# A branch hint for the branch over the general path of a graph network kernel

## The chip, the cores and the metric

The kernel runs on one core of a Trainium2 chip. A core has five engines with a sequencer each: TensorE (PE: matmuls, with its weight loads shown apart as PEld), VectorE (DVE), ScalarE (ACT), GpSimd (POOL) and SyncE (SP, which here only starts DMAs and waits). Each runs its own list of instructions and meets the others through semaphores. [...] The metric is the device time of one execution, in microseconds.

## What is computed

A layer norm with ReLU, then three layers of edge convolution on a graph of 2500 nodes and 80000 edges (the edges are sorted by destination), then one product of all layers' features with a last matrix:

```python
h = relu(layernorm(x))                    # x: 2500 x 256, float32
xs = [h]
for W, b in three layers:                 # W: 512 x 256
    xi, xj = h[dst], h[src]
    m = concatenate([xi, xj - xi]) @ W + b          # one row for each edge
    s = segment_sum(m, dst); cnt = segment_sum(1, dst)
    h = relu(s / maximum(cnt, 1))
    xs.append(h)
out = x + concatenate(xs) @ Wf + bf
```

## The kernel before

The sums over edges are written as products with a matrix of counts, how many edges lead from node m to node n. `by_windows` (line 314) builds this matrix: it takes the destinations in windows of 6 nodes, assumes that a window has at most 256 edges and that a pair of nodes has few edges in common, and compares the edges' node numbers with a running index (`one_m`, `one_n`) to get the counts by matmuls of zeros and ones. The counts go to HBM as bf16 (`a_dram`) for the later layers. Layer 0 is done while the counts are built; layers 1 and 2 stream the counts back (`staged`) and use a scheme of seven products for two pairs of groups of columns. Products that need float32 accuracy are made of two or three reduced products (`zh`, `zl`, `sh`, `sl`, and the forms of `Split` and `Forms`).

The order of the work is written out by hand. A class `InOrder` (line 272) issues through its line 282, so nearly every instruction of the profile has that line; names of tiles tell them apart. At the end (lines 1399 to 1417) ten pairs of node tiles get their last product; VectorE adds it to `acc` (`add_to_acc`), and `out` is written from `acc`, by SP's queue, and twice by ScalarE's, among them the very last write.

The assumptions on the edges may not hold for other inputs. In the first layer VectorE compares the number of edges found with the true one and sets the flag `missing` to 0 or 1. After `by_windows`, `gnn_kernel` loads the flag into a register of every engine (line 1425), each engine branches on it (line 1426), and where it is 1 the whole result is computed anew by `general` (line 17), which assumes nothing. With the inputs of the reference the flag is 0, and no instruction of `general` is in the profile.

In the built program the branch stands behind the last instruction of `by_windows` in the list of each engine. It has two targets: the first instruction of `general`, which comes next in line, and the code behind `general`. The skipped code has 2056 instructions on TensorE, 1780 on VectorE, 275 on ScalarE, 1016 on GpSimd and 139 on SyncE. Behind it each engine has semaphore instructions that end the branch's region (line 1426), and then the closing meeting of all engines (line 1450): each finishes with a DRAIN and reports to GpSimd, which clears the semaphores when all are there.

## Time and profile before

| | us |
|---|---|
| median of three executions | 478.93 (478.14 to 479.45) |
| the profiled execution's own time | 478.33 |
| span of the profile, from the first to the last instruction | 476.4 |
| TensorE busy with matmuls | 463.5 (97%) |
| VectorE busy | 380.9 (80%) |
| ScalarE busy | 310.8 (65%) |
| GpSimd busy | 42.7 (9%) |
| code brought in: 23 packets, 0.38 MB, and 22 packets, 0.18 MB | |

The profile page gives sums and the chain of work that ended last. Instructions of the sequencers alone (branches, register loads, semaphore instructions, DRAINs) are not counted as busy and are not in the chain; a view by source line lists them, with the shortest, median and longest duration in nanoseconds and the first and last start in microseconds from the span's start. A `q` behind an engine's name marks its sequencer or its DMA queue. DMA packets that carry code have the kind "instruction".

### The profile page before, as it was taken

The page shows a single profiled execution, that of the slowest core. Times are in us where ns is not written, and L with a number is a line of the kernel's source. Part 1 is how long each engine was busy: PE and PEld are TensorE (multiplying, and loading weights), DVE is VectorE, ACT ScalarE, POOL GpSimd, SP SyncE. Part 2 cuts the span into 40 slices and gives each one's busy share as a digit, 9 for nine tenths or more (in the row PEclk, how much of TensorE's full clock was granted, in tenths as well). Part 3 has the DMA queues.
Part 4 walks back from the last instruction along what each step waited for, and adds up shares of the span by engine and source line. Part 5 has one row for each costly group of instructions (what it writes and reads, how often), then busy time and mean ns, then how long its engine had stood idle before and what let it go on. Part 6 is the DMA issues. An engine that isn't in the chain of part 4 may idle for free.

```text
span 476.4 us, 7357 instructions
## 1 busy us (share of the span) xinstructions
PE 463.5 (97%) x2739; PEld 365.9 (77%) x2739; DVE 380.9 (80%) x699; ACT 310.8 (65%) x543; POOL 42.7 (9%) x66
## 2 busy tenths in 40 slices
PE   8999999999999999999999999999999999999992
PEld 4787888787877888868887867877788787687691
DVE  8988988799898872599986848876999685669883
ACT  5776687685754441577869858766877886587330
POOL 2664014300101001000000000000000000000000
PEclk9999999999999999999999999999999999999997
DMA  8310084990824608441187542011124764120032
GB/s 279 96 46 1 1 163 70 193 216 14 178 42 89 131 1 179 95 131 43 45 291 258 182 160 89 1 44 45 43 54 158 289 207 151 77 88 0 1 128 95
DMA packets 21779, 52.11 MB, mean 109 GB/s; under 512 B 1943, under 2 KB 12134, under 8 KB 21734
## 3 DMA queue, kind: packets, MB, share of 16 engines
q1 hardware_dynamic: 14662, 33.67, 21.5%
q0 software_dynamic: 5856, 16.51, 18.1%
q10 hardware_dynamic: 1216, 1.37, 0.9%
q8 instruction: 23, 0.38, 0.3%
q14 instruction: 22, 0.18, 0.1%
HBM read 36.08 MB, written 15.46 MB: 108 GB/s over the span
## 4 chain that ended last, share of the span: by engine, by line
PE 86%; DVE 7%; POOL 2%; DMA 2%; issue 1%; SPq 0%; DVEq 0%; POOLq 0%
PE bank L282 82%; PE pz L282 3%; DVE acc L282 2%; DMA acc<-in_x_dram 2%; POOL acc L282 1%; DVE staged L282 1%; DVE st L282 1%; POOL es L282 1%; DVE zl L282 0%; POOL ed L282 0%; DVE mv L282 0%; DVE tmp L282 0%; PE turned L282 0%; DVE rs L282 0%; DVE kn L282 0%
## 5 line engine op out<-in xcount | busy, mean ns | idle before, releaser
L282 ACT CAST block<-staged 128x1008 fp32r<-128x1008 bf16 x120 | 117.8, 1032 | 17.1 <-DVE staged L282 6.3
L282 PE MATMUL bank<-block,zh 128*128 128x504 f32 (+1 forms) x200 | 83.7, 419 | 0.0
L282 PE MATMUL bank<-a,zh 128*128 128x504 f32 (+1 forms) x200 | 81.7, 409 | 0.0
L282 ACT CAST a<-bank 128x480 fp32r<-128x480 f32 (+1 forms) x105 | 54.5, 561 | 39.0 <-PE bank L282 37.1
L282 PE MATMUL bank<-a,zl 128*128 128x504 f32 (+1 forms) x200 | 77.8, 389 | 0.0
L282 PE MATMUL bank<-block,zl 128*128 128x504 f32 (+1 forms) x200 | 77.3, 387 | 0.0
L282 DVE TENSOR_TENSOR one_m<-iota_m,key_m 128x2048 bf16<-128x2048 bf16 (+2 forms) x55 | 64.3, 1169 | 9.9 <-PE bank L282 9.7
L282 PE MATMUL bank<-block,sh 128*128 128x504 f32 x160 | 69.0, 431 | 0.0
L282 PE MATMUL bank<-block,staged 128*128 128x512 f32 (+1 forms) x312 | 67.2, 365 | 0.6 <-DVE staged L282 0.5
L282 PE MATMUL bank<-block,sl 128*128 128x504 f32 x160 | 62.6, 391 | 0.0
L282 PEld LDWEIGHTS bank<-block,staged 128*128 128x128 f32 x312 | 52.3, 188 | 11.9 <-DVE staged L282 2.1
L282 DVE TENSOR_TENSOR one_n<-iota_n,key_n 128x960 bf16<-128x960 bf16 (+2 forms) x110 | 51.4, 508 | 0.0
L282 DVE TENSOR_TENSOR block<-staged 128x1008 fp32r<-128x1008 bf16 x40 | 46.9, 1204 | 5.5 <-PE bank L282 4.2
L282 PEld LDWEIGHTS <-one_m 128*128 128x128 bf16 x834 | 37.4, 97 | 13.6 <-issue 7.6
L282 PEld LDWEIGHTS bank<-block,zh 128*128 128x128 f32 x200 | 37.6, 188 | 10.8 <-issue 2.5
L282 PEld LDWEIGHTS bank<-block,zl 128*128 128x128 f32 x200 | 37.6, 188 | 10.6 <-issue 3.5
L282 PE MATMUL bank<-one_n,one_m 128*128 128x120 bf16 x834 | 44.7, 204 | 0.1
L282 PEld LDWEIGHTS bank<-a,zh 128*128 128x128 f32 x200 | 37.8, 189 | 6.4 <-issue 0.2
L282 PEld LDWEIGHTS bank<-a,zl 128*128 128x128 f32 x200 | 37.8, 189 | 6.3 <-issue 0.2
L282 DVE TENSOR_TENSOR staged<-staged 128x1008 bf16<-128x1008 bf16 x40 | 27.1, 678 | 17.3 <-ACT block L282 16.9
L282 PE MATMUL pz<-wbf,hT 128*128 128x256 f32 x160 | 38.7, 387 | 0.9 <-DMA wbf<-in_L_gnn_Wf_dram 0.7
L282 PEld LDWEIGHTS bank<-block,sh 128*128 128x128 f32 x160 | 30.1, 188 | 10.4 <-issue 3.5
(163 smaller groups left out, 611.8 us busy)
## 6 DMA issues: line engine op xcount, KB each, us to landing
staged<-a_dram SPq DMA_DIRECT2D x52, 504.0 KB, 4.2
a_dram<-a POOLq DMA_DIRECT2D x20, 630.0 KB, 10.8
out_dram<-acc SPq DMA_DIRECT2D x17, 128.0 KB, 1.7
acc<-in_x_dram POOLq DMA_DIRECT2D x3, 640.0 KB
wbf<-in_L_gnn_Wf_dram SPq DMA_DIRECT2D x4, 256.0 KB
acc<-in_x_dram SPq DMA_DIRECT2D x1, 896.0 KB
acc<-in_x_dram ACTq DMA_DIRECT2D x1, 768.0 KB
wbf<-in_L_gnn_W_dram SPq DMA_DIRECT2D x3, 256.0 KB, 6.6
```

Source lines behind the costliest of these rows:

```text
L282: return self.tc.keep_in_program_order(call(*args, **kwargs))
```

## The change

One call is added ahead of `by_windows`, which marks a place for a branch hint under the label `again`, of the kind "likely taken", for TensorE, VectorE and ScalarE; and the branch gets this label. In the built program each of the three engines has one instruction more, a BranchPrefetchHint that names its branch of line 1426, as its first instruction in the kernel. All other instructions stand in the same order as before, and SyncE and GpSimd have the same instructions as before.

```diff
     with tc.tile_pool(name="flag", bufs=1) as flag:
         missing = flag.tile([1, 1], I32, name="missing")
+        tc.mark_branch_hint_location("again", "LikelyTaken",
+                                     engines=[getattr(mybir.EngineType, e) for e in ("PE", "DVE", "Activation")])
         by_windows(tc, x, src, dst, Ws, bs, Wf, bf, out, missing)
         again = nc.values_load(missing, min_val=0, max_val=1)
-        with tc.If(again > 0):
+        with tc.If(again > 0, label="again"):
             general(tc, x, src, dst, Ws, bs, Wf, bf, out)
```

## The prediction

> **What bounds the kernel now.** I read the page first, then the end of the chain of waits, then the instructions of the three lines that end the program (1425 loads the flag, 1426 is the branch, 1450 the closing meeting of all engines), and last the DMA view of the moment of the branch.

> ```profile
> span 476.4 us, 7357 instructions
> q8 instruction: 23, 0.38, 0.3%
> q14 instruction: 22, 0.18, 0.1%
> PE 86%; DVE 7%; POOL 2%; DMA 2%; issue 1%; SPq 0%; DVEq 0%; POOLq 0%
> ```

> TensorE carries 86% of the chain, but the change touches none of its matmuls. What it touches is code loading: the two "instruction" queues. 0.38 MB in 23 packets is 16 KB each, 0.18 MB in 22 is 8 KB each. Code comes in blocks while the kernel runs.

> ```profile
> 0.74 0.45 SPq L282
> 1.24 7.25 DMA acc<-in_x_dram
> 8.52 0.75 DVE st L282 x2
> ...
> 467.95 0.17 DVEq L1425
> 468.13 0.21 DVE acc L282
> ```

> Columns: start, us, what. The chain begins with 7.25 us of loading x, and its last computing instruction ends at 468.3. The span is 476.4: 8.1 us pass after the last result is in SBUF. The chain of waits says nothing of them, since they hold no counted work.

> ```profile
> L1425 ACTq TENSOR_LOAD <-missing x1: 485/485/485, 469.5 to 469.5; - x1
> ...
> L1426 PEldq COMPARE_BRANCH x1: 3942/3942/3942, 466.7 to 466.7; - x1
> L1426 DVEq COMPARE_BRANCH x1: 72/72/72, 468.2 to 468.2; - x1
> L1426 SPq COMPARE_BRANCH x1: 53/53/53, 469.5 to 469.5; - x1
> L1426 ACTq COMPARE_BRANCH x1: 54/54/54, 470.1 to 470.1; - x1
> L1426 DVEq EVENT_SEMAPHORE x1: 21/21/21, 471.3 to 471.3; - x1
> L1426 ACTq EVENT_SEMAPHORE x1: 17/17/17, 473.2 to 473.2; - x1
> ...
> L1450 SPq EVENT_SEMAPHORE x14: 17/28/433, 472.2 to 476.3; - x14
> L1450 SPq DRAIN x3: 7/7/7, 473.3 to 475.8; - x3
> L1450 ACTq DRAIN x2: 8/72/135, 475.4 to 475.8; - x2
> L1450 POOLq EVENT_SEMAPHORE x4: 17/17/17, 475.6 to 476.3; - x4
> ```

> Durations are min/median/max in ns, then first and last start. Each engine executes the branch, then one semaphore instruction behind the general path, then the first DRAIN of the meeting. TensorE's branch lasts 3.94 us; VectorE's lasts 0.07, but its next instruction starts 3.0 us later (468.2+0.07 to 471.3), though its work was done at 468.3; ScalarE's lasts 0.05, and its next starts 3.1 us later (470.1 to 473.2). Then ScalarE needs another 2.2 us (473.2 to 475.4) before its DRAIN. Nobody else is that late: the first DRAIN is at 470.8 on TensorE, 471.4 on VectorE, 473.3 on SP. So ScalarE's branch sets the end: 475.4 + 0.13 = 475.6, where POOL sees the meeting complete, and 0.8 us of closing work follow.

> ```profile
> q8 instruction: 1, 0.02, 18.1%
> ...
> L282 SPq DMA_DIRECT2D out_dram<-acc x18: 286/356/1506, 454.1 to 468.0; - x18
> L282 ACTq DMA_DIRECT2D out_dram<-acc x2: 372/742/1111, 467.6 to 468.4; - x2
> ```

> **The change part by part.** In the built program each of TensorE, VectorE and ScalarE has one new instruction, the hint, as its first in the kernel. Nothing else moves; SP and POOL are the same instruction for instruction. No wait and no DMA is added.

> Head. Three sequencer instructions. No row shows one, so bounds: 0.02 us (a semaphore row, 17 to 21 ns) to 0.59 (the slowest flag load). Nearest is the branch, also an instruction of the sequencer alone: 0.05 to 0.07. They lie before VectorE's memsets, TensorE's warm-up and ScalarE's load of dst. What hides them is the 7.25 us load of x on SP's queue, which the hint doesn't touch. I take 0; with that cover gone 0.07, at most 0.6. Below zero nothing, an added instruction gives no time back.

> ScalarE's branch, 3.1 us. If the hint has the block behind the path loaded beforehand, the semaphore instruction follows the branch as it does where code is present, in some 0.1 us. Bounds: 0 (the hint does nothing) and 3.1. I take 3.0, since the wait is wholly the fetch, and there is time for the fetch: no 8 KB packet starts between 384.7 and 459.1, so ScalarE's last block before the branch was begun over 10 us ahead of it.

> ScalarE's second gap, 2.2 us. An 8 KB packet starts at 473.8, 0.6 after ScalarE arrives in the target block, and its DRAIN starts after that packet: the DRAIN stands in the next block. The hint names one target, so this gap stays: 470.2 + 2.2 = 472.4, and 0.13 for the DRAIN is 472.5. But the added instruction shifts ScalarE's code by one place, and the boundary falls just behind the semaphore instruction: it may vanish. Bounds 0 and 2.2 of gain; worth nothing, because SP is late next.

> SP, next in line. Its DRAIN is at 473.3, after 8 semaphore instructions for DMA landings (to 472.1) and 12 more. The longest, 433 ns against 28, ends right after ScalarE's semaphore instruction of 473.2, whose semaphore it waits for. Without that: 473.3 - 0.4 = 472.9. SP now ends the meeting, gain 475.6 - 472.9 = 2.7 us.

> TensorE's and VectorE's branches, 3.9 and 3.0 us. Their DRAINs at 470.8 and 471.4 are before 472.9: worth nothing by themselves, as ScalarE covers them now and SP then. But TensorE's fetch collides with the last outputs, which SP waits for. Bounds: 0, and 1.15 (1.51 - 0.36). TensorE at its target starts the fetch of the following block: now at 471.3, 0.7 after 470.6; then at about 466.8 + 0.7 = 467.5, nearly where today's fetch is (467.6). So the collision comes back 0.1 us earlier; I take 0.1.

> Sum: 0 + 2.7 + 0.1 = 2.8 us off the profiled execution's 478.33 (span 476.4 and 1.9 around it): 475.5. The median of the runs is 478.93 (478.14 to 479.45), 0.6 above the profiled one; 478.9 - 2.8 = 476.1 is what I predict.

> [...]

> **The rivals.**

> The hint does nothing: the chip doesn't act on it, has lost it after 470 us, or "taken" means the general path, which follows in line anyway. For it: no row shows any fetch out of line before a branch; the hint is given up to 21 code blocks ahead on TensorE. Against: the branch that skips is the taken one (its target had to be fetched), the direction that the hint names. Time 478.9, with the runs' own spread.

> It works and more comes with it: the second gap goes and the outputs land up to 1.15 us earlier. Then SP ends at 472.9 - 1.15 = 471.8, gain 3.8: 475.1.

> Slower: one mechanism. If the place where the next block is brought in ahead is held for the target from the start, the blocks in line are no longer fetched ahead on TensorE. The price of one unfetched crossing in line is ScalarE's 2.2 us; TensorE has about 20 during the kernel. Two cost 4.4, more than the 2.8 saved plus 1.4 (0.3%), and from there it is slower by what can be told; all 20 cost 44 and give 478.9 - 2.8 + 44 = 520. Against it: the hinted target is one block, and today's fetches for the next block start soon after one is entered (0.6 to 0.7 us), so the place seems free most of the time.

> **How the numbers follow.** The hint works: 0.65, of which the variant with more is 0.15; own range 474.8 to 477.0 (gain 3.8 with the profiled execution's 0.6 below the median at one end; at the other ScalarE's bound alone, 2.2, with a slow run). Nothing happens: 0.21, 478.1 to 479.5. Slower by blocks: 0.09; by a dearer head and other small losses over 0.3%: 0.05. What a measurement of this kernel can tell is about 0.3%, 1.4 us. Faster 0.66 (a little from the spread of "nothing"), same 0.20, slower 0.14. The range reaches from 474.8 to 479.2, leaving out the slower cases and the upper edge of "nothing".

> **What would show it.** Right: TensorE's branch row falls from 3942 ns to under 200; ScalarE's semaphore instruction of line 1426 starts within 0.3 us of its branch; SP's long semaphore wait goes from 433 to some 30 ns and its first DRAIN is the last of the first DRAINs, at 472.8 to 472.9; a 16 KB code packet still starts near 467.5; the span is about 473.6. "Nothing" would show the three stalls unchanged. "Slower" would show TensorE idle for some 2 us at block crossings, with "issue" grown in its waits. The prediction is wrong if the hint lapses on ScalarE alone, since only its stall sets the end, or if ScalarE's second gap grows in place of the first: with 3.1 us there, DRAIN 473.3, gain 2.2.

## The result, and the profile after

The changed kernel takes 476.21 us (median of 18 executions, 474.93 to 476.91) against 478.11 for the kernel before in the same comparison (18 executions, 477.14 to 479.45). The ratio is 0.9958, with a 95% interval of 0.9949 to 0.9967: about 2.0 us less (1.6 to 2.4). The profiled execution took 475.84 with a span of 474.0, against 478.33 and 476.4.

The lines around the branch have moved by two: the flag is loaded at 1427, the branch is 1428, the closing meeting 1452. From the page of the changed kernel, its span and the code queues:

```profile
span 474.0 us, 7360 instructions
q8 instruction: 22, 0.36, 0.3%
q14 instruction: 19, 0.16, 0.1%
```

Three instructions more are the hints, and there are four packets of code fewer. From the views by source line of the changed kernel (nanoseconds min/median/max, then first and last start in us):

```profile
L1428 PEldq COMPARE_BRANCH  x1: 398/398/398, 466.5 to 466.5; - x1
...
L1428 ACTq COMPARE_BRANCH  x1: 68/68/68, 470.4 to 470.4; - x1
L1428 ACTq EVENT_SEMAPHORE  x1: 17/17/17, 470.8 to 470.8; - x1
...
L1452 SPq EVENT_SEMAPHORE  x14: 17/28/28, 472.4 to 473.9; - x14
L1452 SPq DRAIN  x3: 7/7/7, 473.1 to 473.4; - x3
...
L1452 ACTq DRAIN  x2: 8/8/8, 470.9 to 473.4; - x2
...
L1452 ACTq BRANCH_PREFETCH_HINT  x1: 50/50/50, 0.7 to 0.7; - x1
```

A hint costs 50 ns at the head. TensorE's branch has fallen from 3942 to 398 ns; VectorE goes from its branch to its semaphore instruction in 0.6 us (468.1 to 468.7) instead of 3.1, ScalarE in 0.5 instead of 3.2. By these times the target's block is there when a hinted engine jumps. When it came the profile doesn't show. Ahead of the branches there are 21 code packets of 16 KB and 16 of 8 KB behind the start of the span in both kernels; what has gone is behind them, where four code packets start instead of eight. But ScalarE's second gap is gone as well: its DRAIN is at 470.9, right behind its semaphore instruction at 470.8, where before 2.2 us lay between them. SP is now the last to meet, at 473.1, and waits for nobody: its longest semaphore instruction is 28 ns instead of 433.

One thing at the end got worse. The first row is again the window 467.5 to 468.0, the others are the issues of the output:

```profile
q8 instruction: 1, 0.02, 20.6%
...
L282 SPq DMA_DIRECT2D out_dram<-acc x18: 286/358/1923, 453.9 to 467.8; - x18
L282 ACTq DMA_DIRECT2D out_dram<-acc x2: 376/952/1529, 467.4 to 468.2; - x2
```

TensorE's 16 KB fetch is still there, 1.2 us behind its branch. It starts 0.3 us after TensorE has arrived at the target, so it is read as the block behind the target. The last two issues of output take 1.92 and 1.53 us, longer than before (1.51 and 1.11). The second of them is ScalarE's own, and ScalarE loads the flag and branches only when it is done: it branches at 470.4, 0.3 us later than before.

Where the time went, from the last addition's end to the end of the span: 8.1 us before (468.3 to 476.4), 5.8 after (468.2 to 474.0). All that the profiles differ by, 2.4 us, is there but for 0.1.

### The profile page after: what moved, and what is told of

Same layout as the page of the kernel before. It is cut to its first block, busy times and chain, and to the rows that moved or that the text cites. A ratio compares the mean times of both kernels' runs of the same rounds, so it can differ in the third digit from the quotient of the medians.

```text
span 474.0 us, 7360 instructions
## 1 busy us (share of the span) xinstructions
PE 463.1 (98%) x2739; PEld 365.6 (77%) x2739; DVE 379.9 (80%) x699; ACT 310.8 (66%) x543; POOL 43.5 (9%) x66
## 4 chain that ended last, share of the span: by engine, by line
PE 86%; DVE 7%; POOL 3%; DMA 2%; issue 1%; ACTq 0%; DVEq 0%; POOLq 0%
PE bank L282 82%; PE pz L282 3%; DVE acc L282 2%; DMA acc<-in_x_dram 2%; POOL acc L282 1%; DVE staged L282 1%; DVE st L282 1%; POOL ed L282 1%; POOL es L282 1%; DVE tmp L282 0%; DVE zl L282 0%; DVE mv L282 0%; PE turned L282 0%; DVE kn L282 0%; DVE rs L282 0%
## 5 line engine op out<-in xcount | busy, mean ns | idle before, releaser
L282 ACT CAST block<-staged 128x1008 fp32r<-128x1008 bf16 x120 | 117.8, 1031 | 17.0 <-DVE staged L282 6.3
L282 PE MATMUL bank<-block,zh 128*128 128x504 f32 (+1 forms) x200 | 83.7, 419 | 0.0
L282 PE MATMUL bank<-a,zh 128*128 128x504 f32 (+1 forms) x200 | 81.7, 409 | 0.0
L282 ACT CAST a<-bank 128x480 fp32r<-128x480 f32 (+1 forms) x105 | 54.4, 561 | 38.7 <-PE bank L282 37.0
L282 PE MATMUL bank<-a,zl 128*128 128x504 f32 (+1 forms) x200 | 77.8, 389 | 0.0
L282 PE MATMUL bank<-block,zl 128*128 128x504 f32 (+1 forms) x200 | 77.3, 387 | 0.0
L282 DVE TENSOR_TENSOR one_m<-iota_m,key_m 128x2048 bf16<-128x2048 bf16 (+2 forms) x55 | 64.3, 1169 | 9.9 <-PE bank L282 9.7
L282 PE MATMUL bank<-block,sh 128*128 128x504 f32 x160 | 68.9, 431 | 0.0
L282 PE MATMUL bank<-block,staged 128*128 128x512 f32 (+1 forms) x312 | 67.2, 365 | 0.6 <-DVE staged L282 0.5
L282 PE MATMUL bank<-block,sl 128*128 128x504 f32 x160 | 62.6, 391 | 0.0
L282 PEld LDWEIGHTS bank<-block,staged 128*128 128x128 f32 x312 | 52.3, 188 | 12.0 <-DVE staged L282 2.1
L282 DVE TENSOR_TENSOR one_n<-iota_n,key_n 128x960 bf16<-128x960 bf16 (+2 forms) x110 | 51.4, 508 | 0.0
L282 DVE TENSOR_TENSOR block<-staged 128x1008 fp32r<-128x1008 bf16 x40 | 47.0, 1205 | 5.5 <-PE bank L282 4.2
L282 PEld LDWEIGHTS <-one_m 128*128 128x128 bf16 x834 | 37.4, 97 | 13.5 <-issue 7.4
L282 PEld LDWEIGHTS bank<-block,zh 128*128 128x128 f32 x200 | 37.6, 188 | 10.8 <-issue 2.5
L282 PEld LDWEIGHTS bank<-block,zl 128*128 128x128 f32 x200 | 37.6, 188 | 10.7 <-issue 3.5
L282 PE MATMUL bank<-one_n,one_m 128*128 128x120 bf16 x834 | 44.7, 204 | 0.0
L282 PEld LDWEIGHTS bank<-a,zh 128*128 128x128 f32 x200 | 37.8, 189 | 6.4 <-issue 0.2
L282 PEld LDWEIGHTS bank<-a,zl 128*128 128x128 f32 x200 | 37.8, 189 | 6.3 <-issue 0.2
L282 DVE TENSOR_TENSOR staged<-staged 128x1008 bf16<-128x1008 bf16 x40 | 27.1, 679 | 17.3 <-ACT block L282 16.9
L282 PE MATMUL pz<-wbf,hT 128*128 128x256 f32 x160 | 38.7, 387 | 0.2 <-ACT hT L282 0.2
L282 PEld LDWEIGHTS bank<-block,sh 128*128 128x128 f32 x160 | 30.1, 188 | 10.4 <-issue 3.5
```

What stands on the lines that cost most here:

```text
L282: return self.tc.keep_in_program_order(call(*args, **kwargs))
```

## The experiments

Two things vanished from ScalarE's end at once, the first stall of 3.1 us and the second gap of 2.2. Either alone could give nearly the whole gain, since SP comes next, 2.3 us before ScalarE's old end. So the first theory (H) is that the hint's early fetch is the gain, and the rival (S, later L) that the gain is the second gap, by where the code lies in its blocks. A third (T) was that TensorE's hint matters through the outputs. All gains are against the kernel before on the same chip, as ratios.

**The hint on ScalarE alone.**

```diff
-        engines=[getattr(mybir.EngineType, e) for e in ("PE", "DVE", "Activation")])
+        engines=[getattr(mybir.EngineType, e) for e in ("Activation",)])
```

> The hint on ScalarE alone; TensorE and VectorE as before. Theory H (the gain is ScalarE's missing fetch): the same gain as the change, 2.0 us (1.6 to 2.4), though TensorE's branch is back at 3.9 us and VectorE's gap at 3.0, since both still report by 471.4 and SP by about 473. Theory T (TensorE's hint matters through the outputs): in the changed kernel TensorE's next-block fetch of 1.65 us made the last output land some 0.3 us later behind the last add; without that hint the gain is 2.3 or more. Theory S (only the shift of ScalarE's code by one instruction matters): 2.0 as well, since ScalarE still has the added instruction.

Measured: 475.59 against 477.81, ratio 0.9946 (0.9932 to 0.9960). That is 2.2 us by the medians and 2.6 by the ratio. TensorE's branch lasts 4.06 us again and VectorE's gap is back at 2.9, and the gain stays: it is that of the whole change within the intervals. T isn't needed, though it isn't ruled out either, as a difference of some tenths can't be seen.

**The hints on TensorE and VectorE only**, the other half of the same edit.

> The hint on TensorE and VectorE, none on ScalarE. H and S: no gain (0, at most 0.4 either way): ScalarE's 3.1 and 2.2 us are back and set the end, while TensorE reports by about 467.6 and VectorE by 468.9. T: a gain or a loss of 0.3 to 1 us by the outputs.

Measured: 475.84 against 477.81, ratio 0.9956 (0.9941 to 0.9972). Both H and S had expected nothing. By source line:

```profile
L1428 ACTq COMPARE_BRANCH  x1: 54/54/54, 470.3 to 470.3; - x1
L1428 ACTq EVENT_SEMAPHORE  x1: 17/17/17, 472.8 to 472.8; - x1
...
L1452 SPq DRAIN  x3: 7/7/7, 472.9 to 473.2; - x3
...
L1452 ACTq DRAIN  x2: 8/8/8, 472.9 to 473.2; - x2
```

ScalarE has no hint and stalls for 2.5 us (470.3 to 472.8), yet its DRAIN follows at once. With the first stall there and the second gap gone the gain is full: it doesn't need the early fetch of H. And S in its first form falls too, as ScalarE's list of instructions is that of before.

**No hint, one more ScalarE instruction early.**

```diff
     ACTo.activation(warm, ones, AF.Sqrt)
+    ACTo.activation(warm, ones, AF.Sqrt)
```

> No hint; instead one more small instruction on ScalarE early in the kernel (the warming activation twice), so that ScalarE's code behind it stands one place later, as in the changed kernel. By the arithmetic of the profile of before the second gap of 2.2 us goes: ScalarE's DRAIN follows its semaphore instruction, at 473.3, and the gain is 2.2 us with the first stall of 3.1 us unchanged (theory S). Theory H in its plain form, that the hint alone makes the gain: 0.

Measured: 475.70 against 477.81, ratio 0.9954 (0.9940 to 0.9968).

```profile
L1427 ACTq COMPARE_BRANCH  x1: 54/54/54, 469.8 to 469.8; - x1
...
L1427 ACTq EVENT_SEMAPHORE  x1: 17/17/17, 472.6 to 472.6; - x1
...
L1451 ACTq DRAIN  x2: 8/8/8, 472.7 to 473.0; - x2
```

A duplicated instruction of 0.2 us, without any hint, gives the whole gain: the first stall stays at 2.8 us and the second gap is gone. That is what the prediction's reading gives, a block's boundary just behind the semaphore instruction that one place of shift removes.

**Three hints, ScalarE as long as before.** One small copy goes from ScalarE to VectorE:

```diff
-        if o == 0:
+        if o == 0 and i == 3:
+            DVEo.tensor_copy(row[:, i:i + 1], pr[:, 0:1])
+        elif o == 0:
             ACTo.copy(row[:, i:i + 1], pr[:, 0:1])
```

> The three hints, but one of ScalarE's small copies (the fourth copy of row) is done by VectorE, so that ScalarE has as many instructions as before and the block boundary lies behind its semaphore instruction again. H: the stall of 3.1 us is gone, the second gap of 2.2 is back, ScalarE's DRAIN is at about 473.0, no later than SP's, and the gain is 1.7 to 2.0 us. S: the gain is gone, 0 to 0.4.

Measured: 476.33 against 477.81, ratio 0.9967 (0.9955 to 0.9979). The gain is there, but the second gap isn't back: semaphore instruction at 471.16, DRAIN at 471.24. So the experiment didn't make the state that it was meant to make, and can't weigh H against S. That again says that with hints it isn't ScalarE's count that decides.

**The kernel before once more**, to see whether the gap is a thing of the program or of one execution.

> The kernel before once more. The profile of before has a second gap of 2.2 us on ScalarE, between its semaphore instruction of line 1426 and its DRAIN. It is missing in the two kernels whose ScalarE has as many instructions as before (hints on TensorE and VectorE alone; hints on all with one copy moved). If the gap is fixed by the program, it is here again, 2.2 us (2.0 to 2.4); if it was chance in one execution, 0.1.

Measured: 477.76 for the profiled execution; ScalarE's semaphore instruction at 472.81 and its DRAIN at 474.97.

```profile
L1426 ACTq EVENT_SEMAPHORE  x1: 17/17/17, 472.8 to 472.8; - x1
...
L1450 ACTq DRAIN  x2: 8/72/136, 475.0 to 475.4; - x2
```

The gap, 2.15 us, belongs to the program.

**The hint on ScalarE alone, every engine with as many instructions as before.** On top of the first experiment's edit:

```diff
-        for step in f.high, f.low, f.across, f.last:
+        for step in f.high, f.low, f.across, lambda: ACTo.activation(parts[2], ws[0][0], AF.Copy, scale=1.0 / C1):
```

> The hint on ScalarE alone, and one of ScalarE's later instructions merged with its neighbour (the last form of the first layer's own weights in one activation instead of two), so that every engine has as many instructions as before. Theory P (the second gap lies where a code block ends, and any change in an engine's number of instructions moves the end away): the second gap is back, 2.2 us, the first stall is 0.4 instead of 3.1, ScalarE's DRAIN is at about 473.0 and SP's at 473.1; gain 1.7 to 2.1 us, all of it the hint's. Theory C (the gap is chance or comes from the other fetches at the end): no gap, SP sets the end at 473.1, gain 2.0.

Measured: 475.40 against 477.62, ratio 0.9949 (0.9932 to 0.9965). No gap again (the semaphore instruction at 470.11, the DRAIN at 470.19), so P in the form of counts falls, but the gap of before is no chance either.

**No hint, one more VectorE instruction.**

```diff
+    DVE.memset(ones, 0.0)
     DVE.memset(ones, 1.0)
```

> No hint; VectorE has one memset more at the start, ScalarE's list is that of before to the instruction. P in the form that ScalarE's own list decides: second gap 2.2 us as before, gain 0 (within 0.3). P in the form that the lists of all engines lie behind one another, so that VectorE's length moves ScalarE's block ends: no second gap, DRAIN at about 472.9, gain 2.0 us without any hint. C: 0 to 2.0.

Measured: 477.62 against 477.62, ratio 0.9994 (0.9984 to 1.0004).

```profile
L1427 ACTq EVENT_SEMAPHORE  x1: 17/17/17, 473.8 to 473.8; - x1
...
L1451 ACTq DRAIN  x2: 8/72/135, 475.9 to 476.3; - x2
```

The gap is there, 2.1 us, with the long DRAIN of 135 ns. One instruction more on VectorE doesn't move ScalarE's gap. What all kernels without the gap have in common is then a hint somewhere, or one ScalarE instruction more.

**The hint on GpSimd alone**, whose branch is passed at 183 us:

```diff
-        engines=[getattr(mybir.EngineType, e) for e in ("PE", "DVE", "Activation")])
+        engines=[getattr(mybir.EngineType, e) for e in ("Pool",)])
```

> The hint on GpSimd alone, whose branch lies at 183 us and sets nothing. The lists of ScalarE, TensorE, VectorE and SP are those of before to the instruction. Theory L (a hint anywhere in the program changes how the loaded code of the other engines lies in its blocks): ScalarE's stall of 2.4 to 3.2 us stays, its second gap goes, SP and ScalarE end together at about 472.9, and the gain is 2.0 us (1.6 to 2.4). Theory N (the second gap went in the kernel with hints on TensorE and VectorE because of their earlier fetches): nothing changes, gain 0 within 0.4.

Measured: 475.67 against 477.68, ratio 0.9955 (0.9941 to 0.9970).

```profile
L1428 PEldq COMPARE_BRANCH  x1: 3722/3722/3722, 466.4 to 466.4; - x1
...
L1428 ACTq COMPARE_BRANCH  x1: 54/54/54, 469.6 to 469.6; - x1
...
L1428 ACTq EVENT_SEMAPHORE  x1: 17/17/17, 472.9 to 472.9; - x1
...
L1452 SPq EVENT_SEMAPHORE  x14: 17/28/640, 471.6 to 473.8; - x14
...
L1452 ACTq DRAIN  x2: 8/8/8, 473.0 to 473.3; - x2
```

Theory L holds. TensorE, VectorE and ScalarE have no hint and all their stalls, SP even waits 0.64 us for ScalarE, and the gain is that of the change: the second gap is gone. ScalarE's instructions are those of before, so the reading is that a hint anywhere changes how the code behind the branch lies in ScalarE's blocks. The code packets agree: behind ScalarE's semaphore instruction the kernel before has two of 8 KB, at 473.84 and 476.38 (the second 0.9 us behind ScalarE's DRAIN), and this kernel has one, at 473.71. By what a hint on another engine does this, no run shows.

**No branch at all.**

```diff
-        again = nc.values_load(missing, min_val=0, max_val=1)
-        with tc.If(again > 0):
-            general(tc, x, src, dst, Ws, bs, Wf, bf, out)
```

> Leaves out the load of the flag, the branch and the general path; the result is by_windows' alone. It bounds what all code fetches at the end cost: no engine jumps. The last outputs' issues take under 0.5 us, the last output lands at about 469.9, SP goes through its semaphore instructions in about 1.1, and the gain is 3.8 to 4.6 us. If it is under 3, the outputs' own landing or the closing meeting sets the end, not the fetches.

Measured: 473.00 against 477.68, ratio 0.9900 (0.9885 to 0.9915), 4.7 us less.

```profile
span 471.2 us, 7325 instructions
...
L282 SPq DMA_DIRECT2D out_dram<-acc x18: 282/341/398, 453.9 to 467.8; - x18
L282 ACTq DMA_DIRECT2D out_dram<-acc x2: 349/354/360, 467.4 to 468.2; - x2
...
L1447 SPq DRAIN  x3: 7/7/7, 470.4 to 470.7; - x3
```

With no code packet behind 466 no issue is long, and SP meets at 470.4. So of the 8.1 us behind the last addition 3.1 remain. The gain is a little over the expected 3.8 to 4.6, and not all of it is code fetches: SP needs 0.3 us from the last landing to its DRAIN, where 1.1 was expected, since the semaphore instructions of the branch's region, eight on SP, are gone as well. The hinted kernel, with SP at 473.1, still pays 2.7 for the branch: its last output lands 3.8 us behind the last addition instead of 1.9, and SP then needs 1.1 us instead of 0.3.

**A late TensorE.** If TensorE's fetch behind the branch holds up the last outputs, let it come when they have left: a matmul of one column that needs VectorE's last addition delays TensorE's branch.

```diff
+    PEo.matmul(bank()[0:1, 0:1], acc[:, t, 0:1], ones, start=True, stop=True)
```

> All three hints, and TensorE gets one small matmul more at the end, of one column of the last tile of acc after VectorE's last addition; its result is not used. TensorE then branches at about 469.0 instead of 466.5, and the fetch of the block behind its target starts at about 470.1 instead of 467.7, when the last outputs have left. If that fetch holds up the last two outputs (their issues took 1.9 and 1.5 us in the changed kernel, against 0.33 to 0.38), the issues fall to under 0.5 us, SP's first DRAIN comes at 471.2 to 471.6 instead of 473.1, and the gain is 3.5 to 4.0 us over before, 1.5 to 1.9 over the changed kernel. If the fetch isn't the cause: the gain of the change, 2.0.

Measured: 475.00 against 477.62, ratio 0.9935 (0.9919 to 0.9951), 2.6 us by the medians and 3.1 by the ratio.

```profile
L1429 PEldq COMPARE_BRANCH  x1: 398/398/398, 469.0 to 469.0; - x1
...
L1453 SPq DRAIN  x3: 7/7/7, 472.2 to 472.5; - x3
...
L282 SPq DMA_DIRECT2D out_dram<-acc x18: 286/342/399, 453.8 to 467.7; - x18
L282 ACTq DMA_DIRECT2D out_dram<-acc x2: 350/363/376, 467.4 to 468.1; - x2
```

The issues are short, so TensorE's fetch was what held them. The other profiles agree: in all ten in which TensorE's 16 KB packet starts between 467.4 and 468.3, an issue of output that starts behind the packet ends 0.3 to 0.4 us after the packet's end. In the kernel with hints on TensorE and VectorE alone the packet starts at 468.33, and there SP's issue of 468.21, just ahead of it, took 0.33 us, while ScalarE's of 468.61 took 1.13. The last output's landing gained less than expected, as SP meets at 472.2, not 471.4. Each output lands in 16 shares: 14 of the last one's land by 470.04, the two others at 470.74 and 471.11, beside the code packets that remain (8 KB each from 469.2, 469.7 and 470.3, 16 KB from 470.2). By its ratio this is the fastest kernel that computes what the reference asks; its interval and that of the change still touch (0.9951 and 0.9949).

**TensorE later still.** The small matmul reads what ScalarE copies behind its last issue:

```diff
+    last = tmps.tile([P, 512], F32, name="tmp")
+    ACTo.copy(last[:, 0:1], acc[:, t, 0:1])
+    PEo.matmul(bank()[0:1, 0:1], last[:, 0:1], ones, start=True, stop=True)
```

> As the kernel with the late TensorE (three hints; gain 2.6 there, with the last share of the last output landing at 471.1 while TensorE's fetch ran from 470.2 to 471.5), but the small matmul reads what ScalarE copies after its last output issue, so TensorE branches some 0.7 us later, at 469.7, and its fetch starts at about 470.9. The last output then lands at 470.3 to 470.7 (VectorE's fetch of 8 KB at 469.2 still holds a share), SP's first DRAIN is at 471.4 to 471.8 instead of 472.2, and the gain over before is 3.0 to 3.4 us. If the last share is held by something else: 2.6 as there.

Measured: 474.93 against 477.68, ratio 0.9943 (0.9929 to 0.9956), 2.7 us less. It can't be told apart from the run above. TensorE's fetch comes at 471.0, behind everything, and two shares of the last output still land late, at 470.74 and 470.94, while two packets of 8 KB run from 469.2 to 469.9. SP meets at 472.0. So it wasn't TensorE's fetch that held the last shares here; what did is not shown.

## Why the prediction was right, and where it wasn't

Predicted 476.1, measured 476.21. The direction and the place are right: the 8 us behind the last result, code fetches behind a jump, the meeting of the engines. That the number fits to 0.1 us is luck, as two errors of some 0.8 us cancel: the gain was forecast at 2.8 and is 2.0, and the kernel before is at 478.11 over 18 executions, where the three shown had 478.93. Two of the signs named for "right" didn't come either: TensorE's branch fell to 398 ns, not under 200, and ScalarE's semaphore instruction starts 0.5 us behind its branch, not within 0.3. And the lower end of the hint's own range, 474.8, doesn't follow from its words: 478.93 less 3.8 and 0.6 is 474.5.

- The head: right. Each hint is some 50 ns, and the last addition ends at 468.2 instead of 468.3.
- ScalarE's first stall: the mechanism is right, 3.1 us fell to 0.4 between branch and next instruction (0.1 was taken). Its worth is wrong. With the second gap gone it is worth nothing that can be measured: the kernels without a hint on ScalarE gain as much (0.9954, 0.9955, 0.9956) as those with one (0.9946, 0.9949, 0.9958, 0.9967). In the kernel with the hint on GpSimd, SP waits 0.64 us for ScalarE, and that is about all that the early fetch could save there.
- The second gap: this is the step that failed. The prediction said that "the hint names one target, so this gap stays", and that its going would be "worth nothing, because SP is late next". It went, and its going alone is enough for the whole gain. The order of the sum hid that: with the first stall taken out first the second is covered by SP, but with the second out first the first is. The prediction named the boundary and the shift that may remove it, and the shift was even enough by itself (one more instruction, no hint, 0.9954); but in the kernels with hints it is not the count. That the early fetch would be worth its 2.3 to 2.7 if the second gap stayed remains arithmetic: no run had a hint and the gap. The prediction's own sign of being wrong fell with it: it said that it would be wrong if the hint lapsed on ScalarE alone, and the kernel with hints on TensorE and VectorE alone is that case, with the full gain (0.9956).
- SP next in line: right. Its wait fell from 433 ns to 28, and it meets last, at 473.1 (said: 472.8 to 472.9).
- TensorE's and VectorE's branches worth nothing by themselves: right, by the kernel without their hints. The term for the collision had the wrong sign: 0.1 of gain was taken. The fetch came back at the place foreseen, in the window from 467.5, but took longer, and the last two issues became 1.92 and 1.53 us. The last share of the last output lands 3.8 us behind the last addition's end, 3.5 before. So the term was 0.4 off, half of the 0.8 us between the forecast gain and the measured one. The other half is the choice of execution: the profiled ones differ by 2.5 us, the medians by 1.9.
- The rival that the hint does nothing is gone: where TensorE has a hint its branch lasts 0.39 to 0.40 us, and 3.6 to 4.2 in the kernels without it. From ScalarE's branch to its next instruction some 0.5 us pass with its hint, and 2.5 to 3.3 without.
- The rival "slower by blocks" is gone: TensorE's 21 packets ahead of its branch stand within 2.3 us of their places before, and the kernel reaches its last addition no later (468.2 against 468.3).

## What to carry to other kernels

When several delays lie one behind the other on the engine that is last, and another engine is close behind, ask for each of them alone what its going would give, in both orders, before one of them gets the whole gain. A change that adds or marks instructions may also act by where the code comes to lie, as ScalarE's second gap of 2.2 us here went with a hint on GpSimd alone. So try the same shift without the change's own effect: here one idle instruction did all that three hints did (0.9954 and 0.9958). And look behind the last computed result: 8.1 us were spent there that no count of busy time and no chain of work showed, and here a fetch of 16 KB of code behind TensorE's branch also held up the last two issues of output: 1.92 and 1.53 us, against at most 0.40 with the fetch later.

## What had not been expected

- A hint on one engine changed the end of another whose own instructions were the same: with the hint on GpSimd alone ScalarE's DRAIN came 0.1 us behind its semaphore instruction instead of 2.2.
- A fetch of 16 KB of code held up the issues of output on two other queues: 1.51 and 1.11 us before, 1.92 and 1.53 after, 0.33 and 0.35 when it came later. One jump on TensorE so delayed data that it had no part in.
- The hinted engine still fetches what is read as the block behind the target 0.3 to 0.6 us after it arrives there, though it needs only a few more instructions. The targets' own packets are gone from the end, and no packet more shows ahead of the branches.
